# A graph layer on one core: where a join's slot numbers are kept, and how many nodes a block's range has

## The chip, the cores and the metric

The kernel runs on one core of one Trainium2 chip. The metric is the time of one execution on the device, in microseconds (us), as the median of several runs. A profile shows one further execution, instruction by instruction.

A core has TensorE (matmuls, shown as PE, its weight loads as PEld), VectorE (DVE), ScalarE (ACT), GpSimd (POOL) and SyncE (SP, which here only issues transfers). They run side by side, each through its own list in order, and wait for each other by semaphores. SBUF is the on-chip memory of 128 partitions; PSUM holds what TensorE writes, in banks; VectorE and ACT read and write both. Transfers between HBM and SBUF run on 16 DMA engines.

## The reference

The graph has 6250 nodes with 64 features and 206,250 edges with 64 features, sorted by destination. Each edge's message goes through two linear layers, messages are averaged by their source node, and a second pair of layers, a projection, a residual and a normalisation follow per node:

```python
row, col = (edge_index[0], edge_index[1])
msg = jnp.concatenate([src_node_features[col], edge_attr], axis=1)
h = jax.nn.relu(msg @ W1a.T + b1a)
h = h @ W1b.T + b1b
sums = jax.ops.segment_sum(h, row, num_segments=n_nodes)
counts = jax.ops.segment_sum(jnp.ones((h.shape[0],), h.dtype), row, num_segments=n_nodes)
agg = sums / jnp.maximum(counts, 1.0)[:, None]
z = jnp.concatenate([src_node_features, agg], axis=1)
z = jax.nn.relu(z @ W2a.T + b2a)
z = z @ W2b.T + b2b
out = jnp.concatenate([z, src_node_features], axis=1) @ Wr.T + br
```

The kernel's result is layernorm(x + out). In it, `row` is `src` and `col` is `dst`, so the first layer needs the features of nodes in sorted order, and the sum goes to nodes in random order.

## The kernel before

**Blocks and windows.** The edges are padded to 1612 tiles of 128 and cut into 124 blocks of 13 tiles (1664 edges). Since `dst` is sorted, a block's edges name a short run of nodes. The kernel allows a range of WIN nodes from the block's first one, called its window (moved down at the end so that it ends with the last node). The first layer of a tile is one matmul with a contraction of WIDE = 64 + WIN rows: 64 rows of edge features and WIN rows of a one-hot that picks the node, against a matrix `mv` of the 64 rows of weights and WIN rows of the window's nodes, already multiplied by their weights. `group(g)` loads a block three steps ahead: the edge features (`in_edgeT`, 64 rows), the edges' places in the window, broadcast to WIN partitions (`in_dst_o` for the first eight blocks, `relt` for the others, 896 bytes twice per row), and the window's WIN rows of `ytab`. `columns` turns places into one-hots: for the first eight blocks on VectorE (L1287), for the others on ACT with a Square (L1280) and a Relu (L1282), where max(0, 1 − d²) is 1 only for d = 0. At the end the kernel looks at whether any place fell outside its window; if so, a flag starts `general_path`, which computes everything again in another way.

**Sorting by source.** Rows of the first layer (`orow`) are written to HBM at places sorted by source. `bins_of`, `counts_of` and `slots` count on VectorE and TensorE how many edges of each group of 128 nodes came before, which gives each edge a row number (`rowidx`); POOL then writes 128 rows with one indirect transfer (`scatter`, L1349). Two steps later at the earliest, rows are read back in stretches that lie in order (`rt`), VectorE makes one-hots of them (L1437), TensorE sums them with matmuls (L1456), and VectorE adds to `part` (L1516).

**The join.** Blocks 8 to 103 treat 6 of their 13 tiles otherwise, in two joins of three tiles. A join sorts its 384 edges into groups of four with the same bin (a quad), and one indirect transfer writes a whole quad per partition (L1321), so that such a block has 7 + 2 indirect transfers in place of 13. For that, `join_bases` and `join_ranks` compute quad numbers with scans on VectorE (L1056, L1060) and matmuls into the PSUM tile `cnt` (L1070 to L1081); `join_at_slots` reduces them by a maximum to the slot number of each edge, six columns (L1092); `marks` compares these with a ramp of 512 and so builds permutation matrices: two of three tiles with one VectorE instruction per join (L1187), the third on ACT with Square and Relu (L1192, L1193), with the slot number as a bias; and `join` multiplies them with `side` (L1222), which holds edge features, the window's one-hot and two more columns, a one and the number in the bin. The result `rj` (L1227) has the features as rows and is what `join_rows` multiplies with `mv` (L1235), whose two last columns pass the one and the number on; ACT applies the Relu into `mrow` (L1238).

**Slot numbers.** They stand in `z_ps`, six columns of the PSUM tile `steady`. The same tile, one bank, holds `ramp` (0 to 127), `in_win` and the words `on`, which VectorE reads in most of its instructions. The bias of an ACT instruction is taken from SBUF, so `marks` first copies the columns that ACT needs from `z_ps` to an SBUF tile `z_act` (L1185). No other ACT instruction of a step reads or writes `steady`.

**Order.** The lists of TensorE, ACT, VectorE and SyncE are in the order in which the program writes them. In step k: VectorE and ACT make the marks of block k; TensorE counts for block k+1 (L1036 to L1049), runs the first layer of four tiles (L1310), then the quad matmuls for k+1 (L1070), which need VectorE's `bases` (L1060), then half a sum, three more tiles, the two joins, `join_rows`, and the rest of the sums. VectorE, after the marks, does `of_quads` and `bases`, the one-hots of k+2, the second half of `side`, the row numbers and slot numbers of k+1, and the one-hots and additions of the sums. POOL takes block k−2, and its transfers wait for given matmuls of step k, so it does not run ahead of the first layer. Five `orow` tiles, six `mrow` tiles and three `marks` tiles go round.

A PSUM tile's bank is guarded as a whole: the program's framework lets two engines follow each other on it, not overlap.

Of the kernel before, what the change touches and what calls it, by code (L numbers as in the profile page):

```python
# [8 lines left out]
F32 = mybir.dt.float32  # L9
# [4 lines left out]
AF = mybir.ActivationFunctionType  # L14
ALU = mybir.AluOpType
# [3 lines left out]
P = 128  # L19
# [428 lines left out]


NG = 13  # L450
WIN = 62
STEP = 43
EPOCHS = (104, 12, 4, 4)
NEAR = 8
# [16 lines left out]
JOIN, QUAD, MARKS, QROWS = 3, 4, 3, 6  # L471
# [3 lines left out]
ON_ACT = 1  # L475
# [3 lines left out]
def order_of(ngr):  # L479


    return [i * STEP % ngr for i in range(ngr)]
# [3 lines left out]
def fast_path(  # L486
# [36 lines left out]
    nc = tc.nc  # L523
    D, N = xT.shape
    H = w1aT.shape[1]
# [10 lines left out]
    JT = 2 * JOIN  # L536
    WIDE = D + WIN
    order = order_of(NGR)
# [12 lines left out]
    def joined(k):  # L551
        if not JOIN_FROM <= k < JOIN_TO:
            return 0
        return 2 if k < TWICE_TO else 1

    def direct(k):
        return BLK - JOIN * joined(k)
# [116 lines left out]
    def lent(i, n):  # L674
        return rt_all.rearrange("p i f -> p (i f)")[:, i : i + n]
# [3 lines left out]
    near_i = const.tile([P, NEAR], I32, name="near_i")  # L679
    nc.sync.dma_start(near_i[D:WIDE, :], first[:NEAR].rearrange("(o g) -> o g", o=1).to_broadcast([WIN, NEAR]))  # L680

# [14 lines left out]
    MV = 4  # L696
    mvs = const.tile([P, MV, W], F32, name="mv")
# [4 lines left out]

    near = lent(2 * NT + NG * P * 3 // 2, NEAR * WIN).rearrange("p (g w) -> p g w", w=WIN)

    spare = lent(2 * NT + NG * P * 3 // 2 + NEAR * WIN, 3 * P).rearrange("p (i q) -> p i q", i=3)
    iota_i = spare[:, 0, :].bitcast(I32)
# [5 lines left out]
    ones = const.tile([P, P], F32, name="ones")  # L712
# [10 lines left out]
    win_i = const.tile([1, NGR], I32, name="win_i")  # L723
    nc.vector.tensor_scalar(win_i, base_i, float(N - WIN), None, op0=ALU.min)

# [11 lines left out]

    ident = const.tile([P, P], F32, name="ident")
    make_identity(nc, ident)
    nc.vector.tensor_copy(mvs[:, :, H:], ident[:, None, WIDE:].to_broadcast([P, MV, 2]))  # L740
    padrow = const.tile([P, PADT * W], F32, name="padrow")
    nc.gpsimd.memset(padrow, 0.0)
    eps = const.tile([P, 1], F32, name="eps")
# [3 lines left out]
    with (  # L747
# [9 lines left out]
        slm = by_slot.enter_context(tc.tile_pool(name="joinp", bufs=4))  # L757
# [23 lines left out]
        def join_top():  # L781
            top.held.close()
            t = Top("join")
            t.marks = [t.tile([P, JOIN, QUAD * P], F32R, f"marks{i}") for i in range(MARKS)]
            t.sides = [t.tile([P, 2, JT, P], F32R, f"side{i}") for i in range(SIDES)]
            t.enats = [t.tile([P, JT, D], F32, f"enat{i}") for i in range(ENATS)]
            t.rjs = [t.tile([P, QUAD * P], F32, f"rj{i}") for i in range(2)]
            t.mrows = [t.tile([P, QUAD, W], F32, f"mrow{i}") for i in range(QROWS)]
            for side in t.sides:
                nc.vector.tensor_copy(side[:, 0, :, WIDE], ones[:, :JT])  # L790
                nc.vector.tensor_scalar(
                    side[:, 1, :, D:], ones[:, None, D:].to_broadcast([P, JT, D]), 0.0, None, op0=ALU.mult
                )
            return t

        def last_top():
# [37 lines left out]
        def places_in_windows():  # L834
            nc.vector.tensor_scalar(at_f, at_i, float(N - WIN), None, op0=ALU.min)
            nc.vector.tensor_scalar(rel, dst_i, at_f, None, op0=ALU.subtract)
            nc.sync.dma_start(relt, rel)
            at_j = hp.tile([P, NGR], F32, name="h_ps")
            nc.vector.tensor_scalar(at_j, top.base, float(N - WIN), None, op0=ALU.min)
            nc.vector.tensor_tensor(  # L840
                rel_j, top.dst, at_j[:, :, None].to_broadcast([P, NGR, JT]), op=ALU.subtract
            )
# [58 lines left out]
        z_ps = steady[:, RAMP + 2 + HALF * T :][:, : 2 * JOIN]  # L901
# [184 lines left out]
        def join_at_slots(k):  # L1086


            g = joined(k)
            t, n = direct(k) + 1, JOIN * g  # L1090
            v = cnt[:, :, HALF * t : HALF * (t + n)].rearrange("p i (b t) -> p t i b", t=n)
            nc.vector.tensor_reduce(z_ps[:, :n], v, axis=mybir.AxisListType.XY, op=ALU.max)  # L1092

        def join_places(k):

# [74 lines left out]

        qtot = const.tile([P, 2 * HALF], F32, name="qtot")

        z_acts = {}

        def marks(k, i):


            m = top.marks[(join_at[k] + i) % MARKS]
            z = z_ps[:, i * JOIN : (i + 1) * JOIN]
            all_q = quad_ramp.rearrange("p g q -> p (g q)")  # L1180
            n = JOIN - ON_ACT
            if i == 0:
                z_act = z_acts[k] = slm.tile([P, 2, ON_ACT], F32, name="z_act")
                g = joined(k)
                nc.scalar.copy(z_act[:, :g], z_ps[:, : g * JOIN].rearrange("p (j t) -> p j t", t=JOIN)[:, :, n:])  # L1185
            z_act = z_acts[k]
            nc.vector.tensor_tensor(  # L1187
                m[:, :n, :], all_q[:, None, :].to_broadcast([P, n, QUAD * P]),
                z[:, :n, None].to_broadcast([P, n, QUAD * P]), op=ALU.is_equal,
            )  # L1190
            for t in range(n, JOIN):
                nc.scalar.activation(m[:, t, :], all_q, AF.Square, bias=z_act[:, i, t - n : t - n + 1], scale=-1.0)  # L1192
                nc.scalar.activation(m[:, t, :], m[:, t, :], AF.Relu, bias=ones[:, :1], scale=-1.0)  # L1193

        def side(k, part_of):
# [45 lines left out]
        for k in range(NGR):  # L1241
            for i in range(joined(k)):
                m = (join_at[k] + i) % QROWS
# [274 lines left out]
        def sum_first(k):  # L1518

            if not marked:  # L1520
                mark()
            g = marked.pop(0)
            g.ps = hp.tile([P, SUMS, H + 1], F32, name="h_ps")
            g.half = range(g.b0, g.b0 + -(-g.nb // 2))
            done[k, "first"] = summed(g.st, g.reads, g.oh, lambda b: g.ps[:, b - g.b0, :], g.half)
            return g
# [17 lines left out]
        for sts in (steps, [*qep.steps, epochs[1].steps[-1]]):  # L1544
            for st, after in zip(sts, sts[1:]):
                grs = groups_of(st)
                n = after.at - st.at
# [57 lines left out]
        for k, ep_ in enumerate(epoch_of):  # L1605

            if k + 3 == JOIN_FROM:
                top = join_top()
# [9 lines left out]
            for i in range(joined(k)):  # L1618
                marks(k, i)
# [78 lines left out]
            g = sum_first(k) if due > 0 else None  # L1698
            if k + 1 < NGR:
                slots(k + 1, counts)  # L1700
            if after:
                join_at_slots(k + 1)
# [214 lines left out]
```

## Time and profile before

| | |
|---|---|
| median of 3 runs | 1891.21 us (1890.05 to 1894.25) |
| the profiled execution | 1890.38 us |
| its span, first to last instruction | 1888.5 us |
| mean clock granted to TensorE | 0.907 |
| instructions | 34037 |
| matmuls; VectorE; ACT instructions | 11427; 2922; 2257 |
| indirect transfers by POOL | 1036 of rows, 192 of quads |
| moved by DMA | 400.19 MB |

How to read the profile: busy time is the time in which an engine worked on an instruction. A group of instructions is shown as line, engine, operation, output<-inputs by the program's names, shapes and count, then busy us and mean ns of one, then the idle time of the engine just before them and what ended it. A wait is written as who waited <- for whom, with total us, times, and longest us; the first name is the waiting instruction. A row of the timeline has start, length, engine and line, with idle time before it in brackets. `z_ps` and `in_win` appear under the name `ramp`, as all of that PSUM tile does, and `rt` stands also for tiles that borrow its memory at the start. A stretch (a row beginning with two times and a colon) gives each engine's busy time with its count, then the granted clock, the mean busy share of the 16 DMA engines, and GB/s. Roughly: until 150 us the first eight blocks, then the join stage to 1400, then blocks without joins to 1750, then the last sums and the node layers.

### The profile page before, as it was taken

The page shows a single profiled execution, that of the slowest core. Times are in us where ns is not written, and L with a number is a line of the kernel's source. Part 1 is how long each engine was busy: PE and PEld are TensorE (multiplying, and loading weights), DVE is VectorE, ACT ScalarE, POOL GpSimd, SP SyncE. Part 2 cuts the span into 40 slices and gives each one's busy share as a digit, 9 for nine tenths or more (in the row PEclk, how much of TensorE's full clock was granted, in tenths as well). Part 3 has the DMA queues.
Part 4 walks back from the last instruction along what each step waited for, and adds up shares of the span by engine and source line. Part 5 has one row for each costly group of instructions (what it writes and reads, how often), then busy time and mean ns, then how long its engine had stood idle before and what let it go on. Part 6 is the DMA issues. An engine that isn't in the chain of part 4 may idle for free.

```text
span 1888.5 us, 34037 instructions
## 1 busy us (share of the span) xinstructions
PE 1539.0 (81%) x11427; PEld 1430.0 (76%) x11427; DVE 1298.0 (69%) x2922; ACT 1078.8 (57%) x2257; POOL 1186.4 (63%) x1245
## 2 busy tenths in 40 slices
PE   3556777777777878888789799889897699999997
PEld 2455666666676777787788788888887598998986
DVE  4346666666656667777778788888875566666787
ACT  1216777777676767677677677677653233323016
POOL 2737777777765666676666666676566666656710
PEclk8668988888888989999899999999998799889999
DMA  3657777765555667667667677777878787787992
GB/s 102 154 173 233 247 235 233 241 215 179 179 169 178 186 184 243 207 201 218 182 209 236 194 221 246 215 224 237 257 221 226 227 248 229 223 238 226 304 279 58
DMA packets 219685, 400.19 MB, mean 212 GB/s; under 512 B 40153, under 2 KB 119365, under 8 KB 219245
## 3 DMA queue, kind: packets, MB, share of 16 engines
q1 hardware_dynamic: 131898, 222.21, 42.3%
q0 software_dynamic: 48512, 120.15, 18.6%
q10 hardware_dynamic: 39090, 55.56, 8.5%
q8 instruction: 93, 1.52, 0.4%
q14 instruction: 92, 0.75, 0.1%
HBM read 220.26 MB, written 177.48 MB: 211 GB/s over the span
## 4 chain that ended last, share of the span: by engine, by line
PE 44%; DMA 20%; ACT 15%; DVE 10%; issue 7%; POOL 3%; SPq 1%; ACTq 0%; POOLq 0%; DVEq 0%
PE h_ps L1456 21%; PE h_ps L1222 10%; DMA rows<-orow,rowidx 6%; PE h_ps L1310 6%; DVE marks L1187 6%; DMA rt<-rows 4%; ACT mrow L1238 4%; POOL rows L1349 3%; DMA rhs<-relt 2%; PE h_ps L1235 2%; DMA rt<-in_xT 2%; ACT marks L1192 2%; ACT rhs L1280 2%; DMA rhs<-in_dst_o 2%; ACT rj L1227 2%
## 5 line engine op out<-in xcount | busy, mean ns | idle before, releaser
L1349 POOL DMA_INDIRECT rows<-orow,rowidx x1036 | 999.6, 965 | 552.0 <-issue 213.2
L1456 PE MATMUL h_ps<-rt,oh 128*128 128x129 f32 x4204 | 548.0, 290 | 57.9 <-issue 37.6
L1456 PEld LDWEIGHTS h_ps<-rt,oh 128*128 128x128 f32 x4204 | 525.9, 205 | 61.8 <-issue 51.2
L1187 DVE TENSOR_TENSOR marks<-quad_ramp,ramp 128x1024 fp32r<-128x1024 f32 x192 | 225.8, 1217 | 283.3 <-ACT z_act L1185 282.2
L1313 ACT ACTIVATE orow<-h_ps 128x384 f32<-128x384 f32 (+1 forms) x304 | 160.3, 529 | 431.5 <-PE h_ps L1310 423.0
L1437 DVE TENSOR_TENSOR oh<-ramp,rt 128x512 f32<-128x512 bf16 (+3 forms) x452 | 329.2, 768 | 66.7 <-DMA rt<-rows 66.2
L1310 PE MATMUL h_ps<-mv,rhs 126*128 126x128 f32 x2072 | 311.5, 299 | 2.0 <-issue 2.0
L1222 PE MATMUL h_ps<-marks,side 128*128 128x512 f32 x1152 | 312.0, 423 | 0.0
L1310 PEld LDWEIGHTS h_ps<-mv,rhs 126*128 126x128 f32 x2072 | 282.0, 211 | 5.5 <-issue 3.7
L1222 PEld LDWEIGHTS h_ps<-marks,side 128*128 128x128 f32 x1152 | 227.9, 205 | 46.3
L1321 POOL DMA_INDIRECT quads<-mrow,qidx x192 | 184.3, 960 | 61.3 <-issue 13.7
L1235 PEld LDWEIGHTS h_ps<-mv,rj 128*128 128x128 f32 x1536 | 194.9, 192 | 30.2 <-ACT mrow L1238 14.0
L1235 PE MATMUL h_ps<-mv,rj 128*128 128x130 f32 x1536 | 199.4, 282 | 18.7 <-ACT mrow L1238 11.3
L1227 ACT COPY rj<-h_ps 128x512 f32<-128x512 f32 x192 | 112.3, 586 | 162.2 <-PE h_ps L1222 162.1
L1070 PE MATMUL cnt_ps<-bases,four_w 128*128 128x150 bf16 x192 | 33.6, 258 | 163.0 <-DVE bases L1060 163.0
L1070 PEld LDWEIGHTS <-four_w 128*128 128x128 bf16 x192 | 19.0, 99 | 177.1 <-issue 176.8
L1193 ACT ACTIVATE marks<-marks,ones 128x512 fp32r<-128x512 f32 x192 | 138.6, 722 | 6.2
L998 DVE TENSOR_TENSOR_SCAN had<-ramp,bins 128x400 bf16<-128x400 bf16 (+1 forms) x124 | 139.1, 1122 | 3.9 <-ACT orow L1617 2.1
L1280 ACT ACTIVATE rhs<-rhs,from_win 62x896 f32<-62x896 bf16 (+1 forms) x116 | 133.1, 1148 | 13.3 <-DMA rhs<-relt 10.4
L1192 ACT ACTIVATE marks<-quad_ramp,z_act 128x512 fp32r<-128x512 f32 x192 | 137.1, 714 | 4.5
L1282 ACT ACTIVATE rhs<-rhs,ones 62x896 f32<-62x896 f32 (+1 forms) x116 | 133.1, 1147 | 2.9
L1516 DVE TENSOR_TENSOR part<-part,h_ps 128x258 f32<-128x258 f32 (+2 forms) x201 | 95.4, 475 | 55.3 <-PE h_ps L1456 54.6
(181 smaller groups left out, 1724.7 us busy)
## 6 DMA issues: line engine op xcount, KB each, us to landing
rt<-rows SPq DMA_DIRECT2D x146, 260.0 KB
rt<-rows SPq DMA_DIRECT2D x80, 390.0 KB
rt<-quads SPq DMA_DIRECT2D x96, 260.0 KB
rhs<-in_edgeT SPq DMA_DIRECT2D x96, 224.0 KB
enat<-in_edgeJ SPq DMA_DIRECT2D x96, 192.0 KB
rows<-orow,rowidx POOLq DMA_INDIRECT x1036
rt<-quads SPq DMA_DIRECT2D x49, 325.0 KB
rows<-padrow ACTq DMA_DIRECT2D x12, 1300.0 KB
```

Of the source, the lines that this page charges most:

```text
L1187: nc.vector.tensor_tensor(m[:, :n, :], all_q[:, None, :].to_broadcast([P, n, QUAD * P]), z[:, :n, None].to_broadcast([P, n, QUAD * P]), op ...
L1192: nc.scalar.activation(m[:, t, :], all_q, AF.Square, bias=z_act[:, i, t - n : t - n + 1], scale=-1.0)
L1222: nc.tensor.matmul(ps, s[:, p, i * JOIN + t, :], m[:, t, :], start=t + p == 0, stop=t == JOIN - 1 and p == 1,)
L1227: nc.scalar.copy(rj, ps)
L1235: done[k, f"join{i}"] = nc.tensor.matmul(ps[:, j, :], rj[:, (g0 + j) * P : (g0 + j + 1) * P], m, start=True, stop=True).ins.name
L1280: nc.scalar.activation(of_win, rel, AF.Square, bias=from_win[D:WIDE, :])
L1310: done[k, c] = nc.tensor.matmul(ps[:, j, :], rhs[:WIDE, of * P : (of + 1) * P], m[:WIDE, :H], start=True, stop=True).ins.name
L1313: nc.scalar.activation(orow[:, k0 : k0 + n, :H], ps[:, :n, :], AF.Relu)
L1321: s = nc.gpsimd.indirect_dma_start(out=qep.rows.rearrange("(q r) f -> q (r f)", r=QUAD), out_offset=bass.IndirectOffsetOnAxis(ap=qidx[:, q ...
L1349: s = nc.gpsimd.indirect_dma_start(out=ep_.rows, out_offset=bass.IndirectOffsetOnAxis(ap=rowidx[:, k % RING * BLK + j : k % RING * BLK + j ...
L1437: nc.vector.tensor_tensor(res[:, at_tile : at_tile + nb * n, :], ramp[:, None, :].to_broadcast([P, nb * n, P]), node[:, :, None].to_broadc ...
L1456: m = nc.tensor.matmul(of_bin(b), oh[:, at_tile, :], rt[:, j * n + t, : H + 1], start=t0 + t == st.lo[b], stop=t0 + t == st.hi[b] - 1,)
```

## The change

Two edits. First, `join_at_slots` reduces the slot numbers into an SBUF tile, six columns from a pool of four buffers, and a VectorE copy writes them from there to `z_ps`. `marks` on VectorE still reads `z_ps`; ACT's Square takes its bias straight from the SBUF tile; the ACT copy is removed. Second, WIN is 60 in place of 62. WIDE becomes 124, the contraction of the first layer 124 rows and that of `join_rows` 128 as before with zeros in the last two, the two extra columns of `side` move to 124 and 125, and the columns behind them are set to zero once, in one instruction more per `side` tile.

```diff
-WIN = 62
+WIN = 60
...
-    nc.vector.tensor_copy(mvs[:, :, H:], ident[:, None, WIDE:].to_broadcast([P, MV, 2]))
+    nc.vector.tensor_copy(mvs[:, :, H:], ident[:, None, WIDE : WIDE + 2].to_broadcast([P, MV, 2]))
...
-                nc.vector.tensor_scalar(
-                    side[:, 1, :, D:], ones[:, None, D:].to_broadcast([P, JT, D]), 0.0, None, op0=ALU.mult
-                )
+                for part_of, c0 in ((0, WIDE + 1), (1, D)):
+                    nc.vector.tensor_scalar(
+                        side[:, part_of, :, c0:], ones[:, None, c0:].to_broadcast([P, JT, P - c0]), 0.0, None,
+                        op0=ALU.mult,
+                    )
...
-            nc.vector.tensor_reduce(z_ps[:, :n], v, axis=mybir.AxisListType.XY, op=ALU.max)
+            z = z_acts[k] = slm.tile([P, JT], F32, name="z_act")[:, :n]
+            nc.vector.tensor_reduce(z, v, axis=mybir.AxisListType.XY, op=ALU.max)
+            nc.vector.tensor_copy(z_ps[:, :n], z)
+
+        z_acts = {}
...
-            if i == 0:
-                z_act = z_acts[k] = slm.tile([P, 2, ON_ACT], F32, name="z_act")
-                g = joined(k)
-                nc.scalar.copy(z_act[:, :g], z_ps[:, : g * JOIN].rearrange("p (j t) -> p j t", t=JOIN)[:, :, n:])
-            z_act = z_acts[k]
...
-                nc.scalar.activation(m[:, t, :], all_q, AF.Square, bias=z_act[:, i, t - n : t - n + 1], scale=-1.0)
+                nc.scalar.activation(m[:, t, :], all_q, AF.Square, bias=z_acts[k][:, i * JOIN + t : i * JOIN + t + 1], scale=-1.0)
```

More of the change, by code (lines that the diff above doesn't have):

```diff
@@ L1171, in fast_path @@
         qtot = const.tile([P, 2 * HALF], F32, name="qtot")
-        z_acts = {}
         def marks(k, i):
```

## The prediction

> **What bounds the kernel now.** I read the page first, then the list of waits, then one ordinary step in the timeline, then the stretches of the span.
>
> ```profile
> span 1888.5 us, 34037 instructions
> ## 1 busy us (share of the span) xinstructions
> PE 1539.0 (81%) x11427; PEld 1430.0 (76%) x11427; DVE 1298.0 (69%) x2922; ACT 1078.8 (57%) x2257; POOL 1186.4 (63%) x1245
> ```
>
> No engine is near full by its busy time, so waits or a hidden floor decide. The waits that touch the edited lines:
>
> ```profile
> DVE marks L1187 <- ACT z_act L1185: 282.2, 79, 8.6
> ...
> PE cnt_ps L1070 <- DVE bases L1060: 163.0, 79, 3.6
> ...
> DVE rhs L1287 <- DMA rhs<-in_dst_o: 67.1, 7, 29.1
> ```
>
> The first two are one chain. One step in the timeline of VectorE, of ACT and of TensorE (start, length, engine, line; in brackets the idle time before it):
>
> ```profile
> 808.48 0.55 DVE L1516 TENSOR_TENSOR part<-part,h_ps 128x387 f32<-128x387 f32 x1
> 810.92 2.35 DVE L1187 TENSOR_TENSOR marks<-quad_ramp,ramp 128x1024 fp32r<-128x1024 f32 x2 [1.90 <-ACT z_act L1185]
> 813.19 0.26 DVE L1056 TENSOR_SCALAR of_quads<-cnt_ps 128x98 bf16<-128x98 f32 x1
> 813.48 0.41 DVE L1060 TENSOR_TENSOR_SCAN bases<-of_quads,even 128x49 bf16<-128x49 bf16 x2
> ```
> ```profile
> 810.73 0.15 ACT L1185 COPY z_act<-ramp 128x2 f32<-128x2 f32 x1
> ```
> ```profile
> 811.57 0.22 PE L1049 MATMUL cnt_ps<-joh,one_w 128*128 128x50 bf16 x1
> 811.61 1.14 PE L1310 MATMUL h_ps<-mv,rhs 126*128 126x128 f32 x8
> 813.95 0.34 PE L1070 MATMUL cnt_ps<-bases,four_w 128*128 128x150 bf16 x2 [1.20 <-DVE bases L1060]
> ```
>
> VectorE is free at 809.03 (808.48 + 0.55) and its slot numbers are its own, yet it stands until ACT has copied z_act at 810.88, which comes late in ACT's order. Its two marks take 2.35 us, so of_quads starts at 813.19 though the counts were there at 811.8, and TensorE stands 1.20 us before L1070.
>
> But POOL sets a second limit. Two rows of its timeline, then five stretches of the span (length; busy us and count of each engine; clock; DMA share, GB/s):
>
> ```profile
> 814.28 0.96 POOL L1349 DMA_INDIRECT rows<-orow,rowidx  x1 [0.30 <-issue]
> ...
> 819.33 0.95 POOL L1349 DMA_INDIRECT rows<-orow,rowidx  x1 [0.30 <-ACT rj L1227]
> ```
> ```profile
> 24.90:158.00 133.10, 72.31 (x377) 64.56 (x376) 59.34 (x98) 31.78 (x69) 76.44 (x78) 0.64 0.57 163
> 158.00:480.00 322.00, 248.32 (x1640) 221.41 (x1639) 206.13 (x533) 246.50 (x511) 244.57 (x254) 0.87 0.69 225
> 480.00:779.00 299.00, 234.91 (x1724) 216.63 (x1722) 197.13 (x480) 206.25 (x430) 193.32 (x202) 0.91 0.62 192
> 779.00:1398.00 619.00, 544.12 (x4297) 509.58 (x4295) 493.71 (x1159) 431.65 (x890) 407.24 (x422) 0.97 0.73 219
> 1398.00:1720.00 322.00, 280.55 (x2099) 267.98 (x2097) 198.69 (x320) 107.18 (x153) 206.68 (x216) 0.88 0.80 231
> ```
>
> Between the two POOL rows lie three more scatters, so four spacings make 5.05 us, 1.262 us each, of which the page counts only 0.96 as busy. Scatters times 1.262 us is POOL's floor, and what is left is the most that a faster TensorE can win: 133.1 − 98.4 = 34.7 in the start, 322 − 320.5 = 1.5 in the first part of the join stage, 299 − 254.9 = 44 in the second, 619 − 532.6 = 86 in the third, 322 − 272.6 = 49 in the tail. So the kernel is bound by POOL's issue from 158 to 480 and by the VectorE/TensorE handshake from 480 to 1398.
>
> **The start and the transfers.** The second edit cuts the rows of every window load from 62 to 60.
>
> ```profile
> 10.00:15.00 5.00, 0.00 (x0) 0.00 (x0) 0.00 (x0) 0.00 (x0) 0.00 (x0) 1.00 0.13 43
> 19.00:24.00 5.00, 2.97 (x14) 2.67 (x13) 3.12 (x4) 0.56 (x1) 0.00 (x0) 1.00 0.13 52
> ```
> ```profile
> rhs<-relt SPq DMA_DIRECT2D x96, 108.5 KB
> ...
> rhs<-in_dst_o SPq DMA_DIRECT2D x8, 403.0 KB
> ```
> ```profile
> 24.91 1.13 POOL L1349 DMA_INDIRECT rows<-orow,rowidx  x1 [21.87 <-ACT orow L1313]
> ```
>
> (Two stretches, two groups of DMA issues, a row of POOL's timeline.) While only the 62-row loads of in_dst_o are under way, the DMA share is 0.13, two engines of 16, at 43 GB/s: 403 KB take 413/43 = 9.6 us. These loads hold VectorE 67.1 us, POOL's first scatter waits to 24.91, and relt's 108.5 KB in each later step go the same way. 62 is 2 × 31; 60 is 4 × 15. By the rows alone the load then uses two engines still (nothing won) to all (9.6 × 2/16 = 1.2 us); I take at least four, 4.8 us, as 60's share with 16.
>
> The Trainium skill, "DMA: Bandwidth & Descriptors", section "Why a DMA increments its semaphore by 16 and not by 1", says that a transfer runs on the largest number of engines up to 16 that divides its slowest dimension: 2 for 62 rows and 15 for 60. The 0.13 above agrees for 62; no run here shows 60. By that rule the load is estimated at 9.6 × 2/15 = 1.3 us, and the sum below would gain some 17 us more in the start (8.3 for the first scatter and the whole 34.7).
>
> **The change part by part.**
>
> ```profile
> L1185 ACT COPY z_act<-ramp 128x2 f32<-128x2 f32 x96 | 14.6, 152 | 16.2 <-DVE oh L1437 16.2
> ```
> ```profile
> L1092 DVE TENSOR_REDUCE ramp<-cnt_ps 128x6 f32<-128x300 f32 x96 | 45.2, 471 | 0.0
> ...
> L1149 DVE SCALAR_TENSOR_TENSOR rowidx<-row,bin_at 128x7 int32<-128x7 f32 x96 | 16.0, 167 | 3.3
> ...
> L1147 DVE COPY tot<-cnt_ps 128x50 f32<-128x50 f32 x4 | 0.8, 201 | 0.0
> ```
>
> 1. The ACT copy goes: 96 × 152 ns = 14.6 us of ACT, which is 57% busy, so nothing by itself; also VectorE's wait on it (and its wait on VectorE, 16.2 us).
> 2. The reduce writes SBUF in place of PSUM: 471 ns for 300 values a lane stays; a store elsewhere is 0, at most ±0.05 × 96 = ±5 us.
> 3. One new VectorE copy of 6 columns a step: no row has it; its price lies between nothing and L1147's 201 ns for 50 columns; nearest is L1149's 167 ns for seven: 96 × 0.167 = 16 us of VectorE. What hides it is VectorE's own 282.2 us of standing. Behind it queue join_places, the one-hots and the next marks. Without that cover it costs 16 us (19 at 201 ns).
> 4. Marks start when VectorE is done with the step before. In the step shown: 809.03 instead of 810.92, end 811.4, of_quads at the counts' end 811.8, bases 0.7 us later at 812.5, before L1310 ends at 812.75. TensorE's 1.20 us is gone. What is late next is POOL, and TensorE's buffers that wait for scatters to land.
> 5. Sixty rows also shorten the window one-hots (two columns fewer of 62) and leave ACT's and TensorE's times, which go by columns. The padding write at the start has one small instruction more per buffer, two in all, under 0.5 us, while POOL and the loads are late anyway.
>
> By stretch, on the path:
> - First scatter: 0 on two engines, 4.8 on four, 8.4 on all; taken 6. Start's POOL slack 34.7: 0 if the loads stay slow, all if they vanish; other large loads remain, so taken 20.
> - 158 to 480: 1.5 at most; 0, though TensorE's waits there shrink: POOL keeps the pace.
> - 480 to 779: 44 at most. TensorE 234.9, VectorE 197.1 and ACT 206.3 lie well under POOL's 254.9, and POOL lags by steps, not within one; taken 38.
> - 779 to 1398: POOL's floor 532.6, TensorE's 544.1, VectorE's 493.7 + 8 of copies. Other waits stay in it:
>
> ```profile
> DVE part L1516 <- PE h_ps L1456: 30.3, 11, 6.8
> DVE of_quads L1056 <- PE cnt_ps L1049: 9.1, 12, 1.0
> ```
>
>  VectorE with these is at 501.7 + 39.4 = 541, so three engines meet near 541 to 544; uneven steps cost perhaps 20 more: 564, gain 55 (0 to 75).
> - Tail, with its share of DMA 0.80 and this wait:
>
> ```profile
> DVE oh L1437 <- DMA rt<-rows: 43.3, 12, 15.4
> ```
>
>  (of 1398 to 1530). If evened-out engines serve the reads sooner, 0 to 30; taken 8, for TensorE is busy 280.6 of 322.
>
> Sum: 6 + 20 + 0 + 38 + 55 + 8 = 127. The span 1888.5 becomes 1761.5; the profiled execution lasted 1.9 us longer than its span (1890.38) and lies 0.8 under the median of 1891.21, so the forecast is 1764 us.
>
> **The rivals.**
> - *POOL and landing times take it back.* With a faster TensorE the buffers of scattered rows (five and six) fill, and waits on landings replace the one removed. For it: POOL is full from 158 to 480 and DMA share is already 0.73. Against: 130 us of POOL slack after 480. Half of the start (13), 20 and 15 of the stages: 48, so 1842 us.
> - *All terms at their best.* 8 + 34.7 + 44 + 75 + 30 = 192: 1698 us. For it, the share of 0.13. The skill's rule above points here; the trace supports its cause for 62 rows.
> - *Slower: the wait stays and the copies come on top.* If marks wait for something else that ends with z_act, VectorE still stands 282.2 us and the copies sit on the path at the end of its order: +16, and 1907 us. It decides where VectorE's standing before marks stays above some 200 us. Against it: marks start 0.04 us after z_act ends (810.88, 810.92), and z_act is ACT's only use of the PSUM bank that VectorE reads all the time. The Trainium skill, "PSUM — Partial Sum Buffer", section "PSUM bank collisions raise a hardware error", has a scheduler order any two engines on one bank, reads too; by that rule the wait goes with the copy, and the trace agrees as far as the two times go.
> - *The window is too small.* Blocks of 61 nodes or more would set the flag and run the general path: 1612 gathers at POOL's 1.262 us alone are 2034 us on top. From the reference's inputs the widest block has 55 nodes (the last one's window is shifted to end at the last node, 60). It decides at 61; hardly possible.
>
> **How the numbers follow.** About 0.2% (4 us) is what a measurement tells from no change. Forecast (between 1720 and 1820): 0.55. Taken back (1820 to 1880): 0.21. Best case (under 1720): 0.14. Slower: 0.07 for the copies, 0.01 for the window. No change, gains and copies cancelling: 0.02. So faster 0.90, same 0.02, slower 0.08. The range reaches from the best case, 1698, rounded to 1700, to just past the first rival, 1848; outside lie the slow cases (0.08), some 0.05 above and 0.05 below.
>
> **What would show it.** Right: no wait of marks on ACT, under 30 us of it in all; L1070's wait under 50; rhs L1287's wait under 30, POOL's first scatter before 20 us; POOL at 1.26 us spacing through 480 to 1398; 96 copies near 0.17 us; TensorE's clock above 0.91 from 480 to 779. Wrong: large new waits of orow or mrow on DMA landings, a DMA share still 0.13 in the start, or VectorE over 95% busy from 779 with TensorE standing behind it.

## The result, and the profile after

The changed kernel takes 1730.97 us (median of 4 runs, 1720.22 to 1740.07) where the kernel before took 1890.63 beside it (4 runs): a ratio of 0.9154, 95% interval 0.9094 to 0.9214. That is 160 us faster, 33 us more than the 127 forecast, and within the range. The profiled execution lasted 1720.22 us, at the fast end of these runs, with a mean granted clock of 0.941 (0.907 before).

The first lines of the page after, and some of its waits, those that answer to the ones shown of before among them (who waited <- for whom: us in total, times, longest us):

```profile
span 1718.2 us, 34171 instructions
## 1 busy us (share of the span) xinstructions
PE 1496.0 (87%) x11427; PEld 1384.3 (81%) x11427; DVE 1314.4 (76%) x3020; ACT 1065.3 (62%) x2161; POOL 1186.3 (69%) x1245
```
```profile
DVE of_quads L1058 <- PE cnt_ps L1051: 100.2, 83, 4.4
...
DVE rhs L1286 <- DMA rhs<-in_dst_o: 20.3, 1, 20.3
...
DVE oh L1436 <- DMA rt<-rows: 18.6, 12, 8.6
...
DVE marks L1186 <- PE h_ps L1221: 3.9, 3, 1.9
...
PE cnt_ps L1072 <- DVE bases L1062: 3.9, 8, 0.9
```

VectorE's 282.2 us before the marks are 3.9 us, and TensorE's 163.0 us before the bases' matmul are 3.9 us. The wait on in_dst_o fell from 67.1 us in seven pieces to 20.3 us in one. VectorE now waits 100.2 us for TensorE's counts, because it comes early; in the step shown next this wait doesn't hold up TensorE. One step after, in the timeline (rows of VectorE and TensorE alone; start, length, engine, line; in brackets the idle time before it):

```profile
715.48 0.55 DVE L1515 TENSOR_TENSOR part<-part,h_ps 128x387 f32<-128x387 f32 x1
715.95 2.34 DVE L1186 TENSOR_TENSOR marks<-quad_ramp,ramp 128x1024 fp32r<-128x1024 f32 x2
...
718.93 0.22 PE L1051 MATMUL cnt_ps<-joh,one_w 128*128 128x50 bf16 x1
718.98 1.14 PE L1309 MATMUL h_ps<-mv,rhs 124*128 124x128 f32 x8
719.19 0.26 DVE L1058 TENSOR_SCALAR of_quads<-cnt_ps 128x98 bf16<-128x98 f32 x1 [0.91 <-PE cnt_ps L1051]
719.49 0.41 DVE L1062 TENSOR_TENSOR_SCAN bases<-of_quads,even 128x49 bf16<-128x49 bf16 x2
...
719.95 0.34 PE L1072 MATMUL cnt_ps<-bases,four_w 128*128 128x150 bf16 x2
```

The marks follow the add of the step before without a gap, of_quads starts when the counts end (719.15), and TensorE goes from L1309 to L1072 without standing. It is the order that point 4 of the prediction worked out.

Two rows for the start, and one for the new copy: a stretch after (length; busy us and count of PE, PEld, DVE, ACT, POOL; clock; DMA share, GB/s), POOL's first scatter, and the copy in the list of groups (count, then busy us and mean ns, then idle time before).

```profile
12.00:15.00 3.00, 2.12 (x10) 2.15 (x11) 2.89 (x5) 0.03 (x1) 0.00 (x0) 1.00 1.02 220
```
```profile
16.44 1.13 POOL L1348 DMA_INDIRECT rows<-orow,rowidx  x1 [13.42 <-DVE rhs L1286]
```
```profile
L1096 DVE COPY ramp<-z_act 128x6 f32<-128x6 f32 x96 | 16.1, 168 | 3.3
```

In this stretch of the start the DMA engines are full (1.02, with other transfers beside the window's), where their share was 0.13; the first scatter comes 8.5 us earlier, and the copy takes 168 ns. Where the rest came from is read by steps. The first count matmul of a step (L1036 before, L1038 after) marks the step's start on TensorE; these are the rows of steps 9, 58, 104 and 123 after:

```profile
104.55 0.31 PE L1038 MATMUL cnt_ps<-had,one_w 128*128 128x200 bf16 x1 [1.89 <-DVE ways L1105]
```
```profile
687.53 0.25 PE L1038 MATMUL cnt_ps<-had,one_w 128*128 128x200 bf16 x1
```
```profile
1259.37 0.31 PE L1038 MATMUL cnt_ps<-had,one_w 128*128 128x350 bf16 x1
```
```profile
1583.96 0.31 PE L1038 MATMUL cnt_ps<-had,one_w 128*128 128x350 bf16 x1
```

| start of step | before | after | gained since the row above | forecast for about this stretch |
|---|---|---|---|---|
| 9 | 156.6 | 104.6 | 52.0 | 26 |
| 36 | 479.5 | 424.0 | 3.5 | 0 |
| 58 | 779.0 | 687.5 | 36.0 | 38 |
| 104 | 1395.1 | 1259.4 | 44.2 | 55 |
| 123 | 1755.1 | 1584.0 | 35.4 | 8 |
| end | 1888.5 | 1718.2 | −0.8 | 0 |

The same stretches after:

```profile
104.00:424.00 320.00, 244.41 (x1647) 210.84 (x1647) 214.59 (x570) 246.54 (x487) 243.31 (x252) 0.90 0.71 223
424.00:687.50 263.50, 229.88 (x1728) 212.70 (x1726) 200.91 (x502) 201.25 (x405) 200.09 (x209) 0.95 0.72 220
687.50:1259.40 571.90, 540.77 (x4273) 506.55 (x4272) 497.37 (x1203) 424.22 (x843) 410.34 (x426) 0.98 0.79 237
1259.40:1584.00 324.60, 298.64 (x2407) 286.42 (x2405) 226.70 (x368) 116.86 (x166) 231.03 (x241) 0.95 0.88 258
```

Taking 1.262 us for each of POOL's scatters, as the prediction did, and adding up what their spacing had beyond that: after its first scatter POOL has 2.0 us of slack up to step 9, 2.5 up to step 36 and 1.5 up to step 58 (35.0, 2.3 and 45.5 before), then 36.6 and 21.2 (87.2 and 56.7 before). So POOL issues without a pause from 16 to 687 us, and it is TensorE's share that is high from there on.

### The profile page after: what moved, and what is told of

Its sections match the earlier page's. It is cut to its first block, busy times and chain, and to the rows that moved or that the text cites. A ratio compares the mean times of both kernels' runs of the same rounds, so it can differ in the third digit from the quotient of the medians.

```text
span 1718.2 us, 34171 instructions
## 1 busy us (share of the span) xinstructions
PE 1496.0 (87%) x11427; PEld 1384.3 (81%) x11427; DVE 1314.4 (76%) x3020; ACT 1065.3 (62%) x2161; POOL 1186.3 (69%) x1245
## 4 chain that ended last, share of the span: by engine, by line
PE 53%; ACT 16%; DMA 13%; DVE 7%; issue 6%; POOL 3%; ACTq 1%; SPq 0%; DVEq 0%; POOLq 0%
PE h_ps L1455 25%; DMA rows<-orow,rowidx 10%; PE h_ps L1309 8%; PE h_ps L1221 8%; PE h_ps L1234 5%; ACT rhs L1279 3%; ACT marks L1191 3%; ACT marks L1192 3%; POOL rows L1348 2%; ACT orow L1312 2%; DVE oh L1436 2%; DMA quads<-mrow,qidx 1%; ACT mrow L1237 1%; ACT rj L1226 1%; DMA rt<-rows 1%
## 5 line engine op out<-in xcount | busy, mean ns | idle before, releaser
L1455 PE MATMUL h_ps<-rt,oh 128*128 128x129 f32 x4204 | 531.5, 285 | 58.2 <-ACT rhs L1279 44.2
L1455 PEld LDWEIGHTS h_ps<-rt,oh 128*128 128x128 f32 x4204 | 509.6, 200 | 61.1 <-ACT rhs L1279 45.4
L1436 DVE TENSOR_TENSOR oh<-ramp,rt 128x512 f32<-128x512 bf16 (+3 forms) x452 | 328.2, 768 | 19.0 <-DMA rt<-rows 18.6
L1309 PE MATMUL h_ps<-mv,rhs 124*128 124x128 f32 x2072 | 299.2, 291 | 2.9 <-issue 2.0
L1221 PEld LDWEIGHTS h_ps<-marks,side 128*128 128x128 f32 x1152 | 211.5, 192 | 78.6 <-ACT marks L1192 38.7
L1309 PEld LDWEIGHTS h_ps<-mv,rhs 124*128 124x128 f32 x2072 | 269.7, 203 | 6.3 <-issue 3.6
L1234 PE MATMUL h_ps<-mv,rj 128*128 128x130 f32 x1536 | 218.6, 295 | 58.8 <-ACT rj L1226 45.1
L1320 POOL DMA_INDIRECT quads<-mrow,qidx x192 | 185.1, 964 | 59.5 <-issue 16.8
L1279 ACT ACTIVATE rhs<-rhs,from_win 60x896 f32<-60x896 bf16 (+1 forms) x116 | 133.2, 1148 | 2.9
L1281 ACT ACTIVATE rhs<-rhs,ones 60x896 f32<-60x896 f32 (+1 forms) x116 | 133.1, 1148 | 2.9
L1237 ACT ACTIVATE mrow<-h_ps 128x260 f32<-128x260 f32 x384 | 122.0, 391 | 14.6 <-PE h_ps L1234 11.0
L1207 DVE TENSOR_TENSOR side<-enat,side 128x384 fp32r<-128x384 f32 x96 | 53.5, 557 | 94.3 <-ACT side L1200 93.0
```

What stands on the lines that cost most here:

```text
L1221: nc.tensor.matmul(ps, s[:, p, i * JOIN + t, :], m[:, t, :], start=t + p == 0, stop=t == JOIN - 1 and p == 1,)
L1234: done[k, f"join{i}"] = nc.tensor.matmul(ps[:, j, :], rj[:, (g0 + j) * P : (g0 + j + 1) * P], m, start=True, stop=True).ins.name
L1279: nc.scalar.activation(of_win, rel, AF.Square, bias=from_win[D:WIDE, :])
L1309: done[k, c] = nc.tensor.matmul(ps[:, j, :], rhs[:WIDE, of * P : (of + 1) * P], m[:WIDE, :H], start=True, stop=True).ins.name
L1320: s = nc.gpsimd.indirect_dma_start(out=qep.rows.rearrange("(q r) f -> q (r f)", r=QUAD), out_offset=bass.IndirectOffsetOnAxis(ap=qidx[:, q ...
L1436: nc.vector.tensor_tensor(res[:, at_tile : at_tile + nb * n, :], ramp[:, None, :].to_broadcast([P, nb * n, P]), node[:, :, None].to_broadc ...
```

## The experiments

Times are medians; "before" is the kernel before on the same chip. Step starts are given as steps 9 / 58 / 104 / 123, in us.

**Each edit alone.** First the slot numbers alone, with the window left at 62 nodes:

```diff
-WIN = 60
+WIN = 62
```

> Only the first edit: slot numbers reduced to SBUF and copied to PSUM, the window stays at 62 nodes. Theory (two edits with separate places): VectorE's standing before marks goes (282 us to under 20), TensorE's wait for bases falls from 163 to under 30; the start is that of before (step 9 near 157 us, first scatter near 25 us) and so is most of the tail; the join stage gives back the 45 + 87 us of POOL's slack after 480 us in large part, about 80: 1810 us, between 1795 and 1830. Rival (the two-engine window loads hold the join stage as well): those loads land too late for the faster loop, waits on relt appear, and the gain is under 40 us: above 1850.

1798.11 us, before 1882.53: ratio 0.9541 (0.9489 to 0.9593). Steps start at 153.6 / 729.2 / 1308.0 / 1659.7. Then the window alone, with the slot numbers kept as before (the diff is against the kernel before; its padding write comes with it):

```diff
-WIN = 62
+WIN = 60
```

> Only the second edit: 60 nodes, slot numbers and ACT copy as before. Theory: the start gains some 52 us (step 9 near 105 us), the tail some 35 us, the join stage keeps its 163 us of TensorE waits for bases and gains at most what an emptier POOL queue gives: 1800 us, between 1785 and 1830. Rival (the tail's 35 us come from TensorE's clock and not from the loads): tail unchanged, 1838 us.

1805.45 us: ratio 0.9564 (0.9509 to 0.962); steps 102.3 / 739.3 / 1349.9 / 1674.6. Waits of the first and of the second kernel:

```profile
DVE oh L1436 <- DMA rt<-rows: 86.5, 41, 14.8
...
DVE rhs L1286 <- DMA rhs<-in_dst_o: 55.6, 5, 27.2
```
```profile
DVE marks L1189 <- ACT z_act L1187: 298.6, 79, 11.8
...
PE cnt_ps L1072 <- DVE bases L1062: 173.5, 79, 10.0
```

The edits gain 84 and 77 us, 161 together, and the changed kernel gains 160: within the spread of the runs they add up. They also share out the stretches. The start belongs to the window alone (step 9 at 102.3 with it, 153.6 without). The window also carries the tail: from step 104 to step 123 the time is 324.7 us with 60 nodes and 351.7 with 62 (324.6 after, 360.0 before). The join stage belongs to the slot numbers: from step 9 to step 104, 1247.6 us with the window alone, 1154.4 with the slot numbers alone, 1238.5 before.

**Is it the bank?** The copy by ACT had carried data that the marks of ACT needed, not those of VectorE. This kernel is the changed one with an ACT copy that nothing reads (its SBUF tile is two columns wider, which the cut leaves out):

```diff
+            if i == 0:
+                nc.scalar.copy(z_acts[k][:, JT:], z_ps[:, :2])
             for t in range(n, JOIN):
```

> The changed kernel with one more ACT copy per step, of two columns of the slot numbers in PSUM into two columns that nothing reads, ahead of ACT's Squares. No result depends on it; it only has ACT read the bank that VectorE reads. Theory (the bank rule makes the wait): VectorE stands before marks again, 250 us or more in all, and the time goes to that of the second edit alone, within 10 us. Rival (the wait came from the data going through ACT's copy): VectorE's wait stays under 30 us and the time is within 10 us of the changed kernel's 1731.

1757.99 us: ratio 0.9307 (0.9247 to 0.9368), 27 us slower than the changed kernel, which neither theory had. The waits show why the edit wasn't the one meant. It stands behind the step's first marks of VectorE, so the copy waits for them, and it is the second marks that wait for the copy:

```profile
DVE marks L1187 <- ACT z_act L1192: 213.1, 95, 11.7
```
```profile
ACT z_act L1192 <- DVE marks L1187: 36.9, 18, 7.8
```

So the copy makes VectorE wait although no data pass, but at a place where the wait costs less: TensorE stands 115.2 us before the bases' matmul, where it was 163.0 before and 3.9 after. The next kernel has the same copy ahead of VectorE's marks, where the kernel before had it:

```diff
+            if i == 0:
+                nc.scalar.copy(z_acts[k][:, JT:], z_ps[:, :2])
             nc.vector.tensor_tensor(
                 m[:, :n, :], all_q[:, None, :].to_broadcast([P, n, QUAD * P]),
```

> The changed kernel, with an ACT copy of two columns of the PSUM slot numbers into SBUF columns that nothing reads, this time ahead of VectorE's marks of the step, where the kernel before had its copy. The theory that the bank alone makes VectorE wait (any two engines on one PSUM bank are put in order, data or not): VectorE's marks stand on this copy for 200 to 300 us in all, L1072's wait on bases is 120 to 180, and the time is that of the run with only the window changed, 1785 to 1825 us. The rival, that only data make it wait and the 27 us of the run before came from the copy's place behind the marks: marks wait under 40 us, the time is 1725 to 1760.

1807.67 us: ratio 0.9595 (0.9507 to 0.9683), the time of the window alone. From step 9 to step 104 it takes 1248.8 us, where the window alone took 1247.6 and the changed kernel 1154.8. The waits are those of before:

```profile
DVE marks L1189 <- ACT z_act L1188: 282.3, 79, 11.6
```
```profile
PE cnt_ps L1072 <- DVE bases L1062: 169.7, 78, 10.0
```

The copy is 14.7 us of ACT (96 of 153 ns). It reads what VectorE's marks also only read, and nothing uses what it writes; yet it brings back all that the first edit gains. So the price was the order that the program keeps between two engines on one bank, not the data and not ACT's 15 us. The Trainium skill, "PSUM — Partial Sum Buffer", section "PSUM bank collisions raise a hardware error", has a compiler's scheduler order any two instructions of different engines that touch the same bank and the same quadrant of 32 partitions, reads too; the order that this kernel's framework keeps agrees, with 282.3 us of standing for a read that shares no data. Whether the chip would need that order can't be told from these runs: a kernel without it was not tried.

**Is it the number of engines?** A window of 57 nodes is narrower than 60, but 57 is 3 × 19.

```diff
-WIN = 60
+WIN = 57
```

> The changed kernel with a window of 57 nodes, 3 x 19. If a transfer runs on the largest number of engines up to 16 that divides its rows, window loads use 3: in_dst_o loads of 57 rows take 57 x 6656 bytes on 3 engines, about 6 us, the start is far slower than with 60 rows (step 9 between 125 and 145 us against 105) and the time about 1760 to 1790. If the count were the common factor with 16, they would use 1 engine: 18 us per load, step 9 beyond 180 us, and the time above 1850. If only the number of rows counted, step 9 stays near 104 us and the time near 1728.

1757.06 us (one run); steps 131.3 / 705.8 / 1280.9 / 1620.7. A stretch with only these loads under way, and the wait on them:

```profile
11.00:14.00 3.00, 0.53 (x2) 0.27 (x2) 0.00 (x0) 0.00 (x0) 0.00 (x0) 1.00 0.19 59
```
```profile
DVE rhs L1286 <- DMA rhs<-in_dst_o: 42.4, 6, 25.8
```

0.19 is three engines of 16. A narrower window is slower than 60, and its start lies between that of 62 rows (153.6) and of 60 (104.6). The Trainium skill, "DMA: Bandwidth & Descriptors", section "Why a DMA increments its semaphore by 16 and not by 1", has a transfer run on the largest number of engines up to 16 that divides its rows: 2, 3 and 15 for 62, 57 and 60. The shares of 0.13 and 0.19 agree. The 1.02 has other transfers in it, so it shows that the 60-row loads are spread, and not that they use 15.

The reverse test keeps the window at 62 nodes and cuts only the transfers (shown for one of the two loads):

```diff
-                s = nc.sync.dma_start(rhs[D:WIDE, :].bitcast(I32), all_of.to_broadcast([WIN, NG * P]))
+                nc.sync.dma_start(rhs[D : D + 60, :].bitcast(I32), all_of.to_broadcast([60, NG * P]))
+                s = nc.sync.dma_start(rhs[D + 60 : WIDE, :].bitcast(I32), all_of.to_broadcast([WIN - 60, NG * P]))
```

> First edit alone (the window stays at 62 nodes), but each load of in_dst_o and relt is issued as 60 rows and then 2 rows. If the second edit's gain is only the engines that a 60-row load goes to: step 9 starts at 100 to 115 us (105 in the changed kernel, 154 with 62 rows in one piece), step 104 to the end takes near 459 us as in the changed kernel, VectorE's oh waits on rt<-rows under 35 us, and the time is 1720 to 1760. If the gain comes from the narrower window itself (columns of the one-hots, bytes): as with the first edit alone, step 9 at 150 and more, the time 1785 to 1815.

1726.63 us: ratio 0.9138 (0.9054 to 0.9221); steps 101.9 / 689.6 / 1262.8 / 1590.7. With 62 nodes, and with 116 + 8 more transfers than the first edit alone, it is as fast as the changed kernel, as far as the spread of the runs tells. So the gain of the second edit is the spread of these two loads; the two columns and the bytes saved, and the load of the window's rows of `ytab`, which still had 62 rows here, are worth nothing that can be told.

**Which load gave the tail?** The changed kernel with relt's loads cut so that they use two engines again, and in_dst_o's left alone:

```diff
-            s = nc.sync.dma_start(
-                rel,
-                relt[g : g + 1, (NG - n) * P :].rearrange("o (h e) -> o h e", h=2).to_broadcast([WIN, 2, half]),
-            )
+            of_all = relt[g : g + 1, (NG - n) * P :].rearrange("o (h e) -> o h e", h=2)
+            nc.sync.dma_start(rel[:58], of_all.to_broadcast([58, 2, half]))
+            s = nc.sync.dma_start(rel[58:], of_all.to_broadcast([WIN - 58, 2, half]))
```

> The changed kernel, but each relt load is issued as 58 rows and then 2 rows, so that by the rule of the start it uses two engines; in_dst_o's loads stay at 60 rows in one piece. Theory, that the start's gain is in_dst_o's and the tail's gain is relt's, whose load on two engines holds up the wide reads: step 9 near 105 us still (100 to 115), VectorE's oh waits on rt<-rows go from 18.6 to 50 and more, step 104 to step 123 takes 345 to 360 us (325 in the changed kernel, 360 before), and the time is 1745 to 1780. The rival, that the tail gained because the clock was granted or because the join ended earlier: 325 to 332 us there, and 1720 to 1745 in all.

1747.37 us: ratio 0.9231 (0.9159 to 0.9304); steps 104.4 / 692.8 / 1271.7 / 1617.8. The start keeps its gain, the join stage almost (from step 58 to step 104 it loses 7 us), and the tail (here: steps 104 to 123) takes 346.1 us in place of 324.6. The medians, 1747 and 1731, are too close to carry the reading alone, since their intervals overlap; the stretch and its waits must. The wait on the wide reads (`rt`) came back, though to 44.1 us in all and not over 50 as expected:

```profile
DVE oh L1435 <- DMA rt<-rows: 44.1, 24, 16.8
```

The tail's stretches of the kernel before, of this one, and of the first edit alone:

```profile
1395.10:1755.10 360.00, 315.44 (x2406) 302.37 (x2404) 228.18 (x368) 119.42 (x170) 230.76 (x241) 0.90 0.81 233
```
```profile
1271.70:1617.80 346.10, 305.14 (x2406) 292.75 (x2406) 227.92 (x368) 116.78 (x166) 230.72 (x241) 0.92 0.85 241
```
```profile
1308.00:1659.70 351.70, 302.96 (x2406) 289.35 (x2404) 228.31 (x368) 116.86 (x166) 230.91 (x241) 0.93 0.81 239
```

What TensorE does not work there (the stretch less its busy time) is 44.6, 41.0 and 48.7 us with relt on two engines. It is 26.0 after, 22.9 with the window alone, 25.9 with loads of 60 and 2 rows, and between 22.8 and 30.7 in all ten traces of this study whose relt loads are spread; with 57 rows, on three engines, it is 35.8. So 10 to 26 us of the tail are relt's, 18.6 between the executions of before and after. The loads of 60 and 2 rows are as many as those of 58 and 2, so it isn't their number. What TensorE does work goes by the clock: 315.4 us at 0.90 before and 298.6 at 0.95 after, for the same matmuls. That part isn't the change's alone: the changed kernel run again and its variant with a split start, in the last runs of this study, had 293.6 us at 0.96 and 315.3 at 0.90 in this stretch:

```profile
1266.10:1590.40 324.30, 293.64 (x2406) 281.42 (x2404) 226.20 (x368) 116.81 (x166) 230.82 (x241) 0.96 0.89 258
```
```profile
1260.80:1598.90 338.10, 315.30 (x2406) 303.29 (x2406) 228.14 (x368) 116.80 (x166) 230.79 (x241) 0.90 0.84 248
```

**The new copy.** Five copies to PSUM a step in place of one:

```diff
-            nc.vector.tensor_copy(z_ps[:, :n], z)
+            for _ in range(5):
+                nc.vector.tensor_copy(z_ps[:, :n], z)
```

> The changed kernel with VectorE's copy to PSUM done five times a step in place of once: 4 x 96 x 0.168 = 64.5 us more of VectorE. Theory, that the copy is hidden while POOL paces the kernel: steps 9 and 58 start within 5 us of the changed kernel (104.6 and 687.5), and some 31 us of copies fall into steps 58 to 104, where VectorE has little left: 10 to 31 us there, the time 1735 to 1770. The rival, that the copy stands on the path of every step, ahead of the marks: 50 to 64 us in all, spread evenly, the time 1780 to 1800. If it is hidden everywhere: 1722 to 1735.

1751.04 us: ratio 0.9225 (0.9151 to 0.9299); steps 106.4 / 693.4 / 1285.8 / 1615.3. Their group:

```profile
L1097 DVE COPY ramp<-z_act 128x6 f32<-128x6 f32 x480 | 80.4, 168 | 16.4
```

64.3 us more of VectorE cost 5.9 us up to step 58, where POOL keeps the pace, and 20.5 us from step 58 to step 104, where 46 steps hold 30.9 us of them. The 5.9 can't be told from nothing: when the changed kernel was run again, step 58 began at 693.7. By that share the one copy of the change costs some 5 of its 16 us, all behind step 58 (an estimate from this run).

**Is POOL the pace?** Small memsets, six ahead of the scatters of a block:

```diff
+            if 8 <= k < 58:
+                for _ in range(6):
+                    nc.gpsimd.memset(lo[:, : NEAR * BLK], 0.0)
```

> The changed kernel with six small POOL memsets (of columns that are no longer read) ahead of the scatters of blocks 8 to 57: 300 of some 0.1 us each, the page's smallest POOL instructions taking 0.088 to 0.125 us, so 26 to 38 us more of POOL. Theory, that POOL's issue of scatters paces the changed kernel up to step 58: step 58 starts 25 to 45 us later than at 687.5 and the time is 1750 to 1775. The rival, that POOL follows the order of TensorE and VectorE and is full by chance: step 58 under 10 us later, the time 1725 to 1740.

1805.86 us: ratio 0.9537 (0.946 to 0.9615). Both numbers expected were missed: the memsets were dearer than estimated. They also all ran early, between 126.7 and 282.8 us, since POOL's list, unlike the other four, isn't kept in the order in which the program is written:

```profile
L1317 POOL MEMSET lo<- 128x104 bf16 x300 | 55.8, 186 | 15.3
```

Between 104 and 430 us the scatters' spacing holds 82 us beyond 1.262 us each. Step 36 starts at 505.2, 81.2 us later than after, and step 58 at 772.0, 84.5 later; the profiled execution ends 90.8 later. So what is added to POOL there comes out at the end nearly one for one, and no later stage makes it up. Nothing was added behind 282.8 us; for the stretch from there to step 58 the argument is POOL's spacing without a pause.

**Can the start still give?** Two transfers of 124 rows at the start (124 is 4 × 31) issued as 112 and 12 rows:

```diff
-                nc.sync.dma_start(relt, rel)
+                for g0, g1 in ((0, 112), (112, NGR)):
+                    nc.sync.dma_start(relt[g0:g1], rel[g0:g1])
```

(and the same for the load of the destinations' rows).

> The changed kernel with the two transfers of 124 rows at the start (the destinations' rows and the write of relt, on four engines by the rule of the start) each issued as 112 and 12 rows. Theory, that POOL is full from its first scatter at 16.4 us on: step 9 within 4 us of 104.6, and no change that can be told, 1718 to 1740. The rival, that the start still waits for these transfers: step 9 at 90 to 98, and 1710 to 1722.

1712.93 us (4 runs, 1710.7 to 1739.6). Step 9 starts at 98.0, 6.6 us earlier, which the theory had not expected. To compare the times on one chip, both kernels were run once more there, six times each:

> The changed kernel unaltered, beside the next run on the same chip: 1720 to 1740 us.

> The kernel with the two 124-row transfers of the start issued as 112 and 12 rows, beside the changed kernel on one chip. Theory, that POOL's pace from 16 us on takes back what the start wins (step 58 began at 689.3 against 687.5): the two medians within 5 us of each other. If the 1713 us of the run before stand for a gain: 10 to 20 us faster than the changed kernel here.

The changed kernel took 1719.77 us (1714.72 to 1734.57; ratio to before 0.9127, 0.9085 to 0.9169), the variant 1730.75 (1714.69 to 1740.18; ratio 0.9162, 0.9114 to 0.9209). The medians are 11 us apart, not the 5 at most that were expected, but the intervals overlap: they can't be told apart. Step 9 starts 6.5 us earlier (98.6 and 105.1), and at step 58 the two are 4.9 us apart (688.8 and 693.7), in the other pair 1.8 us the other way (689.3 and 687.5). POOL's 300th scatter is issued at 398.1 and 398.8 us: TensorE's quicker start doesn't move POOL. No version that beats the changed kernel was found.

## Why the prediction was right, and where it was off

- **The chain of the first edit: right.** The marks' wait was to fall under 30 us, L1070's under 50; both are 3.9. In step order the marks, of_quads and bases stand where point 4 put them. The bank as the cause, argued there from two times 0.04 us apart, is now shown by the copy that passes no data. The slower rival, in which the wait stays, did not come.
- **480 to 779: right.** 38 forecast, 36.0 measured; POOL runs at its spacing there with 1.5 us to spare, and the clock rose to 0.95. The sign "POOL at 1.26 us spacing through 480 to 1398" held only to step 58 at 687.5; from there to step 104 POOL has 36.6 us of slack, and TensorE decides.
- **158 to 480: nearly right.** 0 forecast, 3.5 by TensorE's steps. By POOL's scatters it is nothing: the 100th is issued at 185.1 us before and 143.8 after, the 300th at 438.6 and 398.1, so 41.3 and 40.5 us earlier.
- **The start: mis-sized, 26 for 41 to 52.** The step was "I take at least four" engines, with 6 us for the first scatter and 20 of 34.7 us of slack. The first scatter gained 8.5, the prediction's figure for all engines (8.4) and not that for four (4.8), and POOL's slack gained 33.0, nearly all of it. That sum, 41.5, is the 43 of the best case. TensorE's step 9 gained 52.0, more than POOL: when it began, POOL had issued 77 scatters before and 69 after, and eight spacings of 1.262 us are 10 us.
- **The tail: mis-sized, 8 for 35.4.** The step was "0 to 30; taken 8". The prediction had the mechanism, that evened-out engines serve the wide reads sooner, but weighed it by their wait up to 1530 us alone (43.3 us) and chose near the floor, "for TensorE is busy 280.6 of 322"; a TensorE that stands for its input 44.6 of 360 us has that much to win. Over the whole tail VectorE's wait on these reads went from 60.0 to 13.3 us (rows of before and after, steps 104 to 123), and TensorE's standing fell by 18.6 us.

```profile
DVE oh L1437 <- DMA rt<-rows: 60.0, 20, 15.4
```
```profile
DVE oh L1436 <- DMA rt<-rows: 13.3, 5, 8.6
```

How relt's loads delay the reads is shown only in part. By the packets in the traces (1560 to 3120 bytes each), the wide reads have just one or two packets under way for 69, 51 and 84 us of the tail in the three runs with relt on two engines, and for 29 to 36 us in the changed kernel, its repeat, the window alone and the loads of 60 and 2 rows. That fits reads whose last packets queue behind relt's on two engines. But only 8 to 11 us of VectorE's waits in these three runs fall into such times; how the rest comes about stays open. The other 16.8 of the 35.4 us are TensorE's busy time, which went by the clock of these two executions. The clock didn't follow from less standing: two executions of the kernel with the split start had 0.97 and 0.90 in the tail, with 23.8 and 22.8 us of standing. The prediction had no term for this, so that part of the gain is luck.
- **779 to 1398: right within its bounds, 11 too much.** 55 forecast (0 to 75), 44.2 measured. TensorE's busy time, 540.8 of 571.9 us, is close to the 544 of the prediction. What was put at "perhaps 20" for uneven steps is 31, of which the copy may be 5.
- **The new copy: right.** 168 ns against 167 taken, 16.1 us in all.
- **The rival that takes it back** had one of its signs: ACT's orow L1616 waits 45.6 us in 13 pieces for scatters to land (0.8 before), 39.2 of them between 105 and 424 us. It costs nothing there, since POOL has 2.5 us of slack in that stretch.

Added up, the misses are +26.0, +3.5, −2.0, −10.8, +27.4 and −0.8, 43 us for the profiled execution; against the medians, of which that execution lies 11 us below, it is 33.

## What to carry to other kernels

Look at the DMA share in a stretch where one kind of transfer is alone: in this kernel a share of 0.13 with nothing else running meant two engines of 16. The row count is then the first thing to try: two rows fewer, or the same rows in two transfers, gave 4%. A transfer on few engines is to be priced by every transfer that shares them, not only by whoever waits for it. A read by a second engine of a PSUM bank is to be priced by what the bank's other user then stands for, and by where in the second engine's order it falls: the same copy of 153 ns cost 27 us behind the first marks and about 77 ahead of them.

## What the runs showed of the hardware that was not expected

- The same 2406 matmuls of the tail took TensorE 290.2 us at a granted clock of 0.97 and 315.3 us at 0.90, in two profiled executions of the kernel with the split start. The changed kernel's runs spread over 1.2%, and the prediction's 0.2% was too fine for it: the two kernels at the end of the experiments differ by 11 us and are not told apart.
- A POOL memset of 128 × 104 took 186 ns, where the smallest of the page, of one column, took 88 to 119 ns; among the scatters, 300 of them cost 82 us, 0.27 us each.
- Two stretches measured the engines of a load from its share alone: 0.13 for 62 rows, 0.19 for 57. No stretch holds the 60-row load by itself; with its neighbours the share was 1.02.
